# Layer 1's normalised input kept in memory, denominators gathered before the reciprocal, and small steps moved to ScalarE

## The chip, the cores and the metric

The kernel runs on one core of one Trainium2 chip. The metric is the device time of one execution in microseconds, the median of several runs; lower is better. TensorE (PE), VectorE (DVE), ScalarE (ACT), GpSimd (POOL) and the queue of SyncE (SP), which issues nearly all DMA transfers, each work through their own instructions in order.

## What is computed

The input x has 32 images of 1024 channels, 14 x 14 positions each, in float32. `_gn` is a group norm with 32 groups and no weights.

```python
# layer 0
x = x + conv(_gn(x))      # three codebook stages: scores against 16 centroids, softmax,
                          # a product with a table; each followed by a batch norm _bn;
                          # relu between them, and at the end relu(out + identity)
# layer 1
x = x + attn(_gn(x))
# attn(x):
q = elu(wq @ x[:, :512] + bq) + 1;  k = elu(wk @ x[:, 512:] + bk) + 1
qr, kr = rope(q), rope(k)                     # per head: 16 heads of 64
z = 1.0 / (einsum(q, k.mean(-1)) + 1e-06)     # one denominator per head and position
out = einsum(qr, einsum(kr, x) / n) * z
return out + depthwise3x3(x) + lepe_b         # "lepe"
```

The end of layer 0 is `x + relu(bn3(out3) + gn(x))`: layer 1 begins from x, from the normalised x, and from the third stage's output, once the third batch norm's scale and bias are known.

## The kernel before

Layer 0 (the function `layers`) has three stages. Stage 1 normalises each pair of images on ACT (`normalise`, one piece per 128 channels), from 2 images and all 1024 channels at a time; it keeps only the per-image scale `gn_a` and bias `gn_b`, and not the normalised x. Stage 3 works in 14 chunks of 448 positions (`group(k, n)` computes half of the output channels of a chunk) and stores its output in the DRAM tensor `o3d`; at its end a flag says whether the softmaxes overflowed (then an exact version runs in a branch), and `bn_final` computes scale `sc3` and bias `bi3` of the third batch norm.

Layer 1 works on 16 pairs of images (`pair`). The order of its instructions is written by a planner in the kernel's source (`Plan`): each step is given an engine, a rank, a duration, and what it reads and writes; the planner lists the ready step of the lowest rank on every engine, and its result is a fixed order on each engine. The ranks are sums of the constants in `due`, plus `T` times the number of the pair; they set the order alone. Ring buffers (`ring`) limit how far a pair runs ahead of another: three of `x`, four PSUM banks `mm` for products and transposes, four `pa` for attention outputs.

The steps of a pair, for each half h of the channels (1 serves k, 0 serves q):

- `load`: x, and the third stage's output (`o3q`), from DRAM by SP.
- `front`: for each 128 channels ACT computes the normalised x plus `bi3` (`tb` = `gn_b` + `bi3`; two instructions, one per image, L1680) into a PSUM bank; DVE adds the third stage's output times `sc3` (L1689), then `x + max(.., 0)` (L1694), then takes statistics (L1699).
- `group_norm`: DVE sums the statistics, PE averages over a group with the matrix `gavg` (L1734), DVE subtracts and squares, PE averages again, DVE adds epsilon, POOL computes the power of -1/2 and the products (`scale`, `middle`).
- `normalise`: ACT writes the normalised `y` (L1792) and later the scaled x of the residual with the 3x3 filter's centre (L1792).
- `channels`: the q and k products on PE (L1826), relu and exp on ACT (L1835, L1838), the sum on DVE (L1842), totals of k on ACT (L1846).
- `rope`: four POOL steps for each quarter of q and k (L1870 to L1877).
- `v_tokens`, `k_tokens`, `products`: transposes on PE (L1888), copies by ACT, products k by v (L1925).
- `normalisers`: PE computes the denominators (L1976) in 64 rows, of which 16 are needed; ACT adds 1e-6 (L1985); DVE takes the reciprocal of all 128 x 196 (L1993); SP stores it to `zd` (L1988). `normalise_q` spreads the rows over partitions by four transfers into `zb` (L2005), and POOL multiplies q by them (L2012). The last pair does this with PE instead.
- `attend`: the attention product into the four `pa` banks (L2031); `lepe`: eight filter taps per 128 channels on DVE, into the same bank (L2049), and the addition to x (L2063). In four of eight channel blocks (`SIDES`) one tap is done by ACT (L2078) and POOL (L2086) instead (`side_tap`); in the last pair three, and for six blocks the other five by PE (`diagonal_taps`, L2105).
- `store`: the half's result to the output.

The q and k weights (8 x 512 KB in small pieces, L531 to L534) replace the tables of stage 3 in SBUF, so they are loaded at the start of layer 1, in 24 transfers.

Of the kernel before, what the change touches and what calls it, by code (L numbers as in the profile page):

```python
# [17 lines left out]
P = 128  # L18
# [31 lines left out]

class Plan:
# [31 lines left out]
    def write(self):  # L83
# [6 lines left out]
        engines = {p[0] for p in self.pieces}  # L90
# [59 lines left out]
def conv_preact_kernel(ctx: ExitStack, tc: tile.TileContext, a: dict, out: bass.AP):  # L150
# [18 lines left out]
    o3d = dram.tile([P, CT, NTOK], F32, tag="o3d", name="o3d")  # L169

# [250 lines left out]
    bi3 = cp.tile([P, CT], F32, tag="bi3", name="bi3")  # L421

# [118 lines left out]
    def layers(exact, early=None):  # L541
# [281 lines left out]
        with ExitStack() as s:  # L823
# [40 lines left out]

            first = lambda p: 8 * p - 15 if p > 1 else -99
# [16 lines left out]
            for p in range(NP):  # L882
                for c in range(CT):
                    at(8 * p + c - AHEAD - 1 - (p == 0), normalise(p, c))
            at(24, edges)
# [245 lines left out]
        with ExitStack() as s:  # L1131
# [260 lines left out]
            def group(k, n):  # L1392
# [82 lines left out]
                for i in range(2):  # L1475
                    add(os[i][:, 0], high[i], os[i][:, 0])
                both(lambda i, _, w: term(low[i][:, left], table(two, w), inputs(x4), False))
                both(lambda i, _, w: product(low[i], luts[7][:, w], rows[7], stop=True))
# [7 lines left out]
                for i, m in enumerate(ms):  # L1486
                    add(os[i][:, 1], low[i], os[i][:, 1])
                    nc.sync.dma_start(o3d[:, m :: 4, k * NC : (k + 1) * NC], os[i])
                for i, m in enumerate(ms):
                    stats(m + 4, os[i][:, 1], k, not more)  # L1490
                for f in steps[1:3]:
                    f()
                pending.extend(steps[3:])

            for k in range(1, NCH):
# [6 lines left out]
                group(k, 0)  # L1502
                if check:
                    check = check()
                group(k, 1)
                if check:
                    again = check()
            bn_final(once, None, 3, range(CT), sc3, bi3, mv3)
# [20 lines left out]
    with ExitStack() as s:  # L1529
# [14 lines left out]
        tb = once.tile([P, CT, B], F32, tag="tb", name="tb")  # L1544
        nc.vector.tensor_tensor(tb, gn_b, bc(bi3, 2, B), ALU.add)
# [41 lines left out]
        T = 81.22  # L1587
        SIDES = [0, 3, 4, 7]
        ATT = 2.0
# [9 lines left out]
        tiles["o3q"] = []  # L1599
        for n, k in (("zb", 4), ("e", 2)):  # L1600
            ring(n, k, [P, N2])
# [19 lines left out]
        for n, shape in (  # L1621
            ("gst", [P, 8, 6]),
            ("nmc", [P, 8]),
            ("gd", [P, 8, 2]),
# [11 lines left out]
        def load(p, h, rank):  # L1636
# [14 lines left out]
            if p > 0:  # L1651
                do(SP, rank - 12, 0.9, quad, (), [(xt, c) for c in range(4)], lag=5.0)
            os = []
            for k in range(2):
                ot = Slot("qr" if p == 0 and h == 0 else "o3q")
# [7 lines left out]
                else:  # L1663
                    r = rank - 11 + 8 * k if p > 0 else -99
                    do(SP, r, 0.45, third, (), [(ot, 0), (ot, 1)], lag=4.5)
                os.append(ot)
            return xt, os

        def front(p, h, c, xt, ot, rank):

            ch = 4 * h + c
            w = Slot("pa" if p == 0 and c % 2 else "mm")
            xc = lambda: xt()[:, c]
            o = lambda: ot()[:, c % 2]
            wv = lambda: w()[:, :N2]

            def scaled():
                for i in range(2):
# [5 lines left out]
                        bias=tb[:, ch, b : b + 1],  # L1684
# [8 lines left out]
            def added():  # L1693
                nc.vector.scalar_tensor_tensor(xc(), wv(), 0.0, xc(), ALU.max, ALU.add)  # L1694
# [7 lines left out]
            do(ACT, rank, 0.92, scaled, [xk], [w])  # L1702
            do(DVE, rank, 0.54, third, [ok], [w])
            do(DVE, rank, 0.54, added, [w], [xk])
            do(DVE, rank, 0.56, stats, [xk], [("gst", p % 2, h, c)])

        def warm(n, need):
            pw = Slot("mm")

            def piece():  # L1710
                for _ in range(n):
# [3 lines left out]
                        tb.rearrange("p c b -> p (c b)"),  # L1715
# [4 lines left out]
            do(PE, -50, 0.4 * n, piece, need, [pw])  # L1720

        def group_norm(p, h, rank):
# [10 lines left out]
            def average(ps):  # L1733
                return lambda: nc.tensor.matmul(ps()[:, :8], gavg, g("gs"), start=True, stop=True)  # L1734
# [4 lines left out]
            def centred():  # L1739
                for t in (g("gd"), pd()):  # L1740
                    nc.vector.tensor_tensor(t, mean, bc(pm()[:, :8], 2, 2), ALU.subtract)
                nc.vector.tensor_tensor(pd(), g("gd"), pd(), ALU.mult)
                nc.vector.scalar_tensor_tensor(
                    g("gq"), m2, 1.0 / 98.0, pd(), ALU.mult, ALU.add
                )
                halves(g("gq"))
                nc.vector.tensor_scalar(g("nmc"), pm()[:, :8], -1.0, None, ALU.mult)

            def variance():
                nc.vector.tensor_scalar(g("gve"), pv()[:, :8], EPS, None, ALU.add)  # L1750
# [5 lines left out]
            def middle():  # L1756
# [5 lines left out]
                    v(g("xbi")), v(g("xbi")), bc(lb[:, 4 * h : 4 * h + 4], 2, 2), ALU.add  # L1762
# [4 lines left out]
            do(PE, rank, 0.21, average(pm), [key("gs")], [pm], lag=0.3)  # L1767
            do(DVE, rank, 0.65, centred, [pm, *gst], [key("gs"), key("nmc")])
            do(PE, rank, 0.21, average(pv), [key("gs")], [pv], lag=0.3)
            do(DVE, rank, 0.1, variance, [pv], [key("gve")])  # L1770
            if p == 0 and h == 1:

                for n, need in ((12, []), (9, [key("gve")])):
                    warm(n, need)
# [40 lines left out]
        def channels(p, keys, j, r, t, sums, rank):  # L1815
# [42 lines left out]
            do(ACT, rank - 20, 0.49, relu, [pq], [e])  # L1858
            do(ACT, rank - 20, 0.46, exp, [], [e])
            do(DVE, rank - 20, 0.54, greater, [pq, e], [(t, r)])  # L1860
            if keys:
                do(ACT, rank, 1.08, total, [(t, r)], [(sums, r, j)])
# [457 lines left out]
```

## Time and profile before

| | us |
|---|---|
| median of 3 runs (lowest, highest) | 3338.13 (3337.95, 3338.33) |
| profiled execution, whole | 3338.64 |
| its span, first to last instruction | 3336.5 |
| last product of layer 0 on PE ends | 2267.6 |
| first q or k product of layer 1 | 2306.1 |
| last q or k product of layer 1 ends | 3287.6 |

Busy time of the engines over the whole span: PE 3242.5 us (97%), DVE 2841.2 (85%), POOL 2538.4 (76%), ACT 1787.1 (54%). The 40 slices of the profile are 83 us each; the last 13 are layer 1, where DVE and POOL show 9 tenths and ACT 8 or 9.

A group of instructions is shown as: line, engine, operation, output<-inputs, shapes, count | busy time, mean ns of one | idle time of the engine just before them and what ended it. The mean of one counts from start to end; neighbours overlap, so the distance between starts is shorter. A row of the timeline or the chain begins with its start and length in us. A row of windows gives for each engine the busy time and, in brackets, the number of instructions, then the granted PE clock, the share of the DMA engines and GB/s.

### The profile page before, as it was taken

What the parts mean: (1) busy time and instruction counts of PE and PEld (TensorE: products, weight loads), DVE (VectorE), ACT (ScalarE), POOL (GpSimd) and SP (SyncE); (2) the same over time, 40 slices, a digit from 0 to 9 for tenths busy, and PEclk for the clock granted to TensorE, in tenths of its full rate; (3) what the DMA queues carried; (4) which work ended last, traced back from release to release, by engine and by line L of the source; (5) the groups of instructions that cost most, each with busy time, mean ns of one, the idle gap of its engine ahead of it and who ended that gap; (6) DMA issues with size and microseconds to landing.
All of it is one profiled execution on the core that took longest, in us unless ns stands there. A gap on an engine that the chain in (4) does not pass through costs nothing. (4 is left out here: it accounts for less than half of the span.)

```text
span 3336.5 us, 60995 instructions
## 1 busy us (share of the span) xinstructions
PE 3242.5 (97%) x22169; PEld 1974.6 (59%) x22169; DVE 2841.2 (85%) x4191; ACT 1787.1 (54%) x4435; POOL 2538.4 (76%) x1590
## 2 busy tenths in 40 slices
PE   8999999999899999999999999997999999999998
PEld 4555555555354444444478888885666666666665
DVE  8999999997788899888666666754699999999996
ACT  5555555554444444444321111104898898898886
POOL 6999999997788888888532222222989999999998
PEclk9999999999999999999999999998999999999999
DMA  4110110102444444343221111114133333333331
GB/s 122 47 49 28 47 47 28 47 28 77 137 127 119 116 119 125 110 127 107 77 71 50 40 60 48 50 50 116 55 85 95 98 88 93 99 92 89 98 91 40
DMA packets 260493, 266.32 MB, mean 80 GB/s; under 512 B 52077, under 2 KB 258965, under 8 KB 260185
## 3 DMA queue, kind: packets, MB, share of 16 engines
q1 hardware_dynamic: 259488, 262.02, 27.2%
q8 instruction: 178, 2.92, 0.4%
q14 instruction: 131, 1.07, 0.1%
q10 hardware_dynamic: 696, 0.31, 0.0%
HBM read 171.01 MB, written 75.58 MB: 74 GB/s over the span
## 5 line engine op out<-in xcount | busy, mean ns | idle before, releaser
L660 POOL TENSOR_TENSOR t<-t,r 128x1568 f32<-128x1568 f32 (+3 forms) x288 | 961.5, 3339 | 521.2 <-issue 244.5
L780 PE MATMUL po<-t,lut 128*128 128x392 f32 x3840 | 1332.5, 500 | 7.4 <-DMA t<-spare 6.4
L780 PEld LDWEIGHTS po<-t,lut 128*128 128x128 f32 x3840 | 710.7, 190 | 606.6 <-issue 82.5
L1826 PE MATMUL mm<-y,lut 128*128 128x392 f32 x2048 | 706.9, 496 | 4.6 <-DVE k L1842 3.5
L622 DVE STREAM_TRANSPOSE tt<-t 128x1568 f32<-128x1568 f32 (+1 forms) x284 | 517.4, 1822 | 155.0 <-ACT t L610 149.7
L610 ACT ACTIVATE t<-sc,cbias 128x392 f32<-128x392 f32 (+1 forms) x624 | 322.0, 597 | 559.0 <-PE sc L943 187.6
L1826 PEld LDWEIGHTS mm<-y,lut 128*128 128x128 f32 x2048 | 375.6, 188 | 268.3 <-DVE k L1842 10.6
L653 DVE STREAM_TRANSPOSE r<-rc 128x1568 f32<-128x1568 f32 (+1 forms) x284 | 520.8, 1834 | 11.6 <-POOL t L660 1.2
L2049 DVE SCALAR_TENSOR_TENSOR pa<-y,lepe_w,pa 128x406 f32<-128x406 f32 x900 | 527.7, 635 | 2.1 <-PE pa L2031 1.9
L625 POOL TENSOR_TENSOR tt<-tt 128x784 f32<-128x784 f32 x256 | 470.5, 1838 | 31.6 <-DVE tt L622 31.6
L610 ACT ACTIVATE t<-sc,room 128x392 f32<-128x392 f32 x512 | 258.7, 588 | 395.6 <-issue 168.4
L1406 PE MATMUL po<-t,lut 128*128 128x224 f32 (+2 forms) x1352 | 313.3, 414 | 0.0
L641 DVE TENSOR_REDUCE sm<-tt 128x98 f32<-128x784 f32 (+1 forms) x284 | 293.6, 1034 | 1.1 <-POOL tt L625 0.8
L1406 PEld LDWEIGHTS po<-t,lut 128*128 128x128 f32 (+1 forms) x1352 | 233.4, 189 | 62.9 <-issue 60.2
L643 DVE RECIPROCAL rc<-sm 128x98 f32<-128x98 f32 (+1 forms) x284 | 220.1, 775 | 9.8
L664 ACT ACTIVATE sm<-sm 128x98 f32<-128x98 f32 (+1 forms) x284 | 85.3, 300 | 154.8 <-DVE rc L643 154.8
L1680 ACT ACTIVATE mm<-x,tb,gn_a 128x196 f32<-128x196 f32 x248 | 126.9, 516 | 48.8 <-POOL y L1559 28.4
L2012 POOL TENSOR_TENSOR qr<-qr,zb 128x784 f32<-128x784 f32 x64 | 118.3, 1862 | 37.2 <-DMA zb<-zd 37.2
L1838 ACT ACTIVATE e<-e 128x392 f32<-128x392 f32 x256 | 133.5, 521 | 0.7
L1073 PE MATMUL sc<-patch,room 27*32 27x392 f32 x4096 | 122.7, 505 | 8.7 <-DMA patch<-h1d 8.7
L1419 DVE TENSOR_TENSOR o<-po,o 128x224 f32<-128x224 f32 (+1 forms) x156 | 81.6, 543 | 56.7 <-PE po L1406 51.9
L854 ACT ACTIVATE x<-x,gn_b,gn_a 128x196 f32<-128x196 f32 x256 | 127.6, 559 | 0.0
(211 smaller groups left out, 4379.3 us busy)
## 6 DMA issues: line engine op xcount, KB each, us to landing
patch<-h1d SPq DMA_DIRECT2D x383, 108.5 KB
x<-in_x_dram SPq DMA_DIRECT2D x32, 784.0 KB
o3d<-o SPq DMA_DIRECT2D x56, 448.0 KB
x<-in_x_dram SPq DMA_DIRECT2D x64, 392.0 KB
out_dram<-x SPq DMA_DIRECT2D x64, 392.0 KB
o<-o3d SPq DMA_DIRECT2D x62, 392.0 KB
h1d<-pad SPq DMA_DIRECT2D x96, 225.0 KB
patch<-h1d SPq DMA_DIRECT2D x383, 54.2 KB
```

Of the source, the lines that this page charges most:

```text
L610: nc.scalar.activation(t[:, j, : sc.shape[1]], sc, AF.Identity if exact else AF.Exp, bias=bias[:, j : j + 1],)
L622: nc.vector.transpose(tt, tf)
L625: nc.gpsimd.tensor_tensor(tv[:, :, :8], tv[:, :, :8], tv[:, :, 8:], ALU.add)
L641: nc.vector.tensor_reduce(sm, tv, AX.X, ALU.add)
L643: nc.vector.reciprocal(rc, sm)
L653: nc.vector.transpose(r, bc(rc, 2, KC))
L660: nc.gpsimd.tensor_tensor(v[:, c], v[:, c], r[:, c], ALU.mult)
L780: nc.tensor.matmul(po[h], luts[b][:, j, h * P : (h + 1) * P], ts[u % len(ts)][:, j, :N2], start=(b == 0 and j == j0), stop=(b == 7 and j = ...
L1406: nc.tensor.matmul(dst, w, x, start=start, stop=stop)
L1826: nc.tensor.matmul(pv(), w[kt][:, m0 : m0 + P], ywin(p, first + kt), start=(kt == 0), stop=(kt == 3),)
L1838: nc.scalar.activation(e(), e(), AF.Exp, scale=-1.0)
L2049: nc.vector.scalar_tensor_tensor(acc, neighbours(p, c, offset(k)), lw[:, c, k : k + 1], acc, ALU.mult, ALU.add,)
```

## The change

1. Stage 1 of layer 0 also stores the normalised x of pairs 1 to 15 in a DRAM tensor `gnd` (`keep`, 60 transfers of 392 KB by SP). Layer 1 loads it (`kept`, four transfers a pair into a ring `gn` of four) in place of recomputing it with ACT; only pair 0 still does that. `third` adds into the SBUF tile.
2. `bi3` is no longer added to the input of the relu: `x + max(v, -bi3)` is formed, which is the wanted value less `bi3`. Group norm takes account of it by one more matmul per mean (`centring`, L1813 of the new kernel), and `lbi` = `lepe_b` + `bi3` puts it back into the residual.
3. In group norm the square, the negated mean and the added epsilon go from DVE to ACT; one copy of the differences goes.
4. Denominators: ACT's result is stored to `zr`; a transfer gathers the 16 rows that count as 128 x 49 (`zc`); DVE takes the reciprocal of that; it is stored to a smaller `zd`, from which the four spreads are made as before.
5. In pairs before the last, three channel blocks in place of four have a side tap: one tap per pair goes from ACT and POOL back to DVE. The last pair's split is as before.
6. At the end of layer 0 the last chunk's sums are finished in another order with the flag read in between, and scale and bias of the third batch norm are computed in two halves (`last_bn`), nearly all on POOL.
7. All ranks (`due`, `T`) and some durations that the planner assumes are new, several steps have ranks of their own, the k weights come ahead of the `o3d` loads at the start, and the planner goes through the engines in a fixed order. 11 idle matmuls instead of 21 stand at the start (`warm`).

```diff
+            def keep(p, c):
+                def piece():
+                    nc.sync.dma_start(
+                        gnd[:, c - 1 : c + 1, p * N2 : (p + 1) * N2], xts[p][:, c - 1 : c + 1]
+                    )
+                return piece
...
                     at(8 * p + c - AHEAD - 1 - (p == 0), normalise(p, c))
+                    if p > 0 and c % 2:
+                        at(8 * p + c - AHEAD, keep(p, c))
...
+            def last_bn(n):
...
+                nc.vector.tensor_scalar(ve, four(mv3[:, :, 1]), EPS, None, ALU.add)
+                half = mhalf[:, :4].rearrange("p (h m) -> p h m", h=2)
+                nc.gpsimd.tensor_tensor(sc, ve, half, ALU.pow)
+                nc.gpsimd.tensor_tensor(sc, sc, four(g), ALU.mult)
+                nb = four(nbi3)
+                nc.gpsimd.tensor_tensor(ve, four(mv3[:, :, 0]), sc, ALU.mult)
+                nc.gpsimd.tensor_tensor(nb, ve, four(b), ALU.subtract)
+                nc.gpsimd.tensor_tensor(bi, four(b), ve, ALU.subtract)
...
-        tb = once.tile([P, CT, B], F32, tag="tb", name="tb")
-        nc.vector.tensor_tensor(tb, gn_b, bc(bi3, 2, B), ALU.add)
+        nc.vector.scalar_tensor_tensor(centring, gavg, 2.0, ident, ALU.mult, ALU.subtract)
+        nc.gpsimd.tensor_tensor(lbi, lb, bi3, ALU.add)
...
-        SIDES = [0, 3, 4, 7]
+        SIDES = [5, 6, 7]
...
+                def kept(gt=gt, q=q):
+                    nc.sync.dma_start(gt(), gnd[:, 2 * q : 2 * q + 2, p * N2 : (p + 1) * N2])
...
-                nc.vector.scalar_tensor_tensor(xc(), wv(), 0.0, xc(), ALU.max, ALU.add)
+                nc.vector.scalar_tensor_tensor(
+                    xc(), wv(), nbi3[:, ch : ch + 1], xc(), ALU.max, ALU.add
+                )
...
-            do(ACT, rank, 0.92, scaled, [xk], [w])
+            if p == 0:
+                do(ACT, rank, 0.92, scaled, [xk], [wk])
...
             def centred():
-                for t in (g("gd"), pd()):
-                    nc.vector.tensor_tensor(t, mean, bc(pm()[:, :8], 2, 2), ALU.subtract)
-                nc.vector.tensor_tensor(pd(), g("gd"), pd(), ALU.mult)
...
-                nc.vector.tensor_scalar(g("nmc"), pm()[:, :8], -1.0, None, ALU.mult)
+                nc.vector.tensor_tensor(pd(), mean, bc(pm()[:, :8], 2, 2), ALU.subtract)
+            def squared():
+                nc.scalar.activation(pd(), pd(), AF.Square)
+                nc.scalar.activation(g("nmc"), pm()[:, :8], AF.Copy, scale=-1.0)
...
-                nc.vector.tensor_scalar(g("gve"), pv()[:, :8], EPS, None, ALU.add)
+                nc.scalar.activation(g("gve"), pv()[:, :8], AF.Identity, bias=eps)
...
+            do(SP, rank + due["z"], 0.45, keep, ["z"], [("zr", p % 2)], lag=2.3)
+            do(SP, rank + due["z"], 0.45, gather, [("zr", p % 2)], ["zc"], lag=2.3)
+            do(DVE, rank + due["z"], 0.4, recip(zc), [], ["zc"])
+            do(SP, rank + due["z"], 0.45, scatter, ["zc"], [("zd", p % 2)], lag=2.3)
...
-            do(SP, b - 90, 0.95, weights4[b], (), [("w", b)], lag=3.5 + b)
+            do(SP, b - (110 if b < 4 else 90), 1.85, weights4[b], (), [("w", b)], lag=4.5)
```

## The prediction

> **What bounds the kernel now.** I read the busy shares of the 40 slices first, to find the stage that the change touches (layer 1, from 2270 us to the end), then the chain of waits to see its rhythm, then one period of it by engine.
>
> In the chain of waits (start, length, what):
>
> ```profile
> 2579.94 18.71 PE mm L1826 x56
> 2603.07 4.94 DVE pa L2049 x9
> ...
> 2632.67 4.39 DVE pa L2049 x8
> 2637.59 2.20 DVE pa L2049 x4
> 2641.94 18.72 PE mm L1826 x56
> ```
>
> The same pattern returns every 62.0 us, once for each pair of images, and the chain changes between PE (the q and k products, L1826) and DVE (the 3x3 taps, L2049). The busy time of each engine in the next period:
>
> ```profile
> core 0: us, PE busy (x) PEld busy (x) DVE busy (x) ACT busy (x) POOL busy (x), PEclk, DMA share, GB/s
> 2641.94:2703.93 61.99, 60.39 (x616) 39.01 (x617) 60.87 (x134) 55.01 (x138) 57.60 (x55) 1.00 0.34 94
> ```
>
> DVE is idle for 1.1 us of 62.0, PE for 1.6. So two engines bound the period; taking 8 us from ACT alone buys nothing here. The groups of that period which the change touches:
>
> ```profile
> L1680 ACT ACTIVATE mm<-x,tb,gn_a 128x196 f32<-128x196 f32 x16 | 8.2, 516 | 0.3
> L1689 DVE SCALAR_TENSOR_TENSOR mm<-o,sc,mm 128x392 f32<-128x392 f32 x8 | 5.0, 622 | 0.0
> L1694 DVE SCALAR_TENSOR_TENSOR x<-mm,x 128x392 f32<-128x392 f32 x8 | 4.4, 554 | 0.0
> L2086 POOL TENSOR_TENSOR x<-x,side 128x392 f32<-128x392 f32 x4 | 4.1, 1026 | 0.6 <-ACT side L2078 0.6
> L1993 DVE RECIPROCAL z<-z 128x196 f32<-128x196 f32 x1 | 1.4, 1370 | 0.0
> L1734 PE MATMUL mm<-gs,gavg 128*128 128x8 f32 x8 | 1.3, 240 | 0.0
> ```
>
> The start of the stage, in order of time:
>
> ```profile
> 2277.91 1.07 ACT L1680 ACTIVATE mm<-x,tb,gn_a 128x196 f32<-128x196 f32 x2 [28.41 <-POOL y L1559]
> 2289.18 0.17 DVE L1737 TENSOR_REDUCE gs<-gst 128x8 f32<-128x16 f32 x1
> 2294.10 0.20 POOL L1754 TENSOR_TENSOR gb<-nmc,ga 128x8 f32<-128x8 f32 x1
> 2299.11 0.52 ACT L1680 ACTIVATE mm<-x,tb,gn_a 128x196 f32<-128x196 f32 x1 [13.20 <-DMA x<-in_x_dram]
> 2305.05 3.62 ACT L1792 ACTIVATE y<-x,gb,ga 128x196 f32<-128x196 f32 x8
> 2306.13 15.80 PE L1826 MATMUL mm<-y,lut 128*128 128x392 f32 x40
> ```
>
> Scale and bias of the first half are ready at 2294.3, but y, which uses them, starts at 2305.05: ahead of it in ACT's queue stands L1680 for the second pair, which waits 13.2 us for that pair's x. PE's products start at 2306.1.
>
> The path of the denominators:
>
> ```profile
> 2673.11 1.37 DVE L1993 RECIPROCAL z<-z 128x196 f32<-128x196 f32 x1
> 2674.51 0.34 SPq L1988 DMA_DIRECT2D zd<-z  x1
> 2676.35 2.36 SPq L2005 DMA_DIRECT2D zb<-zd  x4
> 2681.76 1.85 POOL L2012 TENSOR_TENSOR qr<-qr,zb 128x784 f32<-128x784 f32 x1 [1.69 <-DMA zb<-zd]
> ```
>
> **The period, part by part.** ACT: the 16 L1680 go (-8.2), one side tap goes (-0.6, as four channels become three), six small steps of group norm come: about 0.25 each, between nothing and the 0.30 of the smallest ACT row (L664, 98 elements), +1.5. 55.0 becomes 47.7; never the bound. POOL loses one L2086: 57.6 - 1.0 = 56.6.
>
> DVE: one tap more, 0.55 (eight L2049 start 4.38 us apart in all). Of group norm, gd, its product, nmc and gve go; their starts in the timeline lie 0.08, 0.22, 0.07 and 0.07 apart, 0.44, twice: -0.9. The reciprocal works on 49 elements a partition instead of 196: the rows with 98 (775 ns) and 196 (1370 ns) give 6.1 ns an element, so 0.48 us: -0.9. L1689 now reads and writes SBUF instead of PSUM: between 622 and the 554 of L1694, which writes SBUF; I take none of the 0.5 us. 60.9 + 0.55 - 0.9 - 0.9 = 59.6 us. In the written order the two halves between attentions now hold equal DVE work (29.8 and 29.7 us by these durations; before 29.8 and 30.9), and taps stand where DVE waited 0.6 us for the group mean.
>
> PE: two more means per pair (`centring` times `bi3`). Four L1734 means take 1.3 us, 0.33 each: +0.65, between +0.3 (weights already loaded beside) and +0.7. 60.4 becomes 61.05. This speaks against the change, and makes PE the bound.
>
> Here a rule differs from the row. The Trainium skill, "Trainium Kernel Development and Optimization", section Best Practices, says that matmul busy time does not tell the distance from the roofline. The trace agrees in part: 56 L1826 take 18.7 us, 2.67 for eight, while eight followed by other work are booked at 2.9, so some of PE's 60.4 is no work. By the row PE ends at 61.05 or more; by the rule PE can shrink, DVE stays the bound, and the period is 59.6 + 1.1 = 60.7. Upper end: PE keeps its 1.6 us of idle, 62.65. I take 61.3, near the row with little idle, since DVE has 1.7 us of slack to deliver in time. 0.7 us in each of 15 periods: **-10.5 us** (rule -20; upper end +10).
>
> The denominators travel further: ACT's z is stored (zr), gathered (zc), inverted, stored (zd), then spread: two hops more on SP's queue. A store with its wait takes 1.84 us here (2674.51 to 2676.35), the spread 5.4 (2676.35 to 2681.76). The gather isn't in the trace: its pieces are 196 B, and "DMA: Bandwidth & Descriptors", section Specifications, says that below 512 B a transfer isn't at line rate. That rule is against the change. By the row it costs 1.9, by the rule perhaps twice that; the weight loads at 2280 us have pieces of 128 to 256 B and moved 264 GB/s, so I take 2.2. From the end of the denominators' product: 1 + 1.9 + 2.2 + 0.7 + 1.9 + 5.4 = 13 us. In the new order POOL's first L2012 stands behind the first two products of the next pair's k (11.1 us of PE work later, then 2 of ACT and DVE) and 4.9 of POOL work: 18 us. So the detour is covered by rope work, and POOL's present wait of 2.7 us goes. Without that cover it would cost 5 us a pair. Behind these waits on SP stand two `gn` loads, the stores and the next x, which have some 20 us. Price taken: 0. The four `gn` loads per pair, 1.6 MB in 61 us, add 26 GB/s to 94: hidden.
>
> **The first layer.** 60 stores of 0.4 MB (`keep`), 24 MB over the first 1000 us, where 59 GB/s flow and PE is busy for 98%. Each stands behind `t<-spare` on SP, one unit after the normalise that it waits for; what is queued behind is needed four units later. 0, at most +3.
>
> The end of layer 0: the last chunk's first half finishes its sum earlier, and `last_bn` takes one POOL chain (1.65 + four of 0.2) instead of POOL and three DVE steps after the statistics; the flag is read before them. From the last product (2267.6) to bi3 it took 6.3 us; I get 4.8. **-1.5**.
>
> **The start.** x of the second pair is no longer in ACT's queue. The first half's four channels now stand alone on DVE: 4 x 1.7 us from 2277.5, gs at 2284.4; 4.6 us more for the group norm (4.9 before, a little DVE work left out, two hops to ACT put in), y at 2289.5, first product at 2290 instead of 2306; the k weights (2.1 MB at 0.27 MB/us from 2278, now all ahead of the o3 loads) are there at 2288. But then DVE is late: in its order the first k result stands behind `gn` of the second pair, and the second behind its x, which on SP now come after 6.6 and 8.2 MB: 2303 and 2309. Four PSUM buffers fill, and the products wait. Following those queues, the first q product starts near 2325; before it was 2331.4 (2328.8 and one group of 2.64). **-5** beyond the 1.5; between +4 (the loads later by 9 us) and -14 (16 us kept).
>
> **The end.**
>
> ```profile
> 3244.39 1.53 POOL L1870 TENSOR_TENSOR kr<-k,cosq 128x784 f32<-128x784 f32 x1 [0.30 <-DVE k L1842]
> 3320.68 1.90 POOL L2012 TENSOR_TENSOR qr<-qr,zb 128x784 f32<-128x784 f32 x1
> 3329.97 1.03 DVE L2063 TENSOR_TENSOR x<-mm,x 128x392 f32<-128x392 f32 x2
> ```
>
> From the last pair's k rope to 3322.6 POOL never rests (78 us); DVE's last ten taps and the store follow. In the new order those taps come earlier, POOL's own work from that point is 77.8 us, with four side taps last; only additions and the 5.5 us of the store follow: 7 saved. But that k rope stands 4.5 us later against the products' end. **-2**, between -7 and +4.
>
> **Sum**, against the profiled execution (span 3336.5, 3338.64 with what lies around it): -1.5 - 5 - 10.5 - 2 = -19. 3338.6 - 19 = 3319.6; the runs' median is 0.5 lower, so **3319 us**.
>
> **Rivals.**
> - *Only the start and end gain* (chance 0.2): PE keeps 0.9 us of idle, the period stays at 62.0. For: PE gets more work, and its order is fixed. Against: DVE, which it waited for, has 1.3 us less. -8.5: 3330 us.
> - *Slower: the denominators' detour decides* (0.18). Each of the three new-style hops on SP costs 6 us instead of 2. The 13 us become 25; 18 are covered and POOL has 4.7 us of slack in 61.3. It decides from 5.2 us a hop on; at 6, 2.3 us a pair, 15 times: 3319 + 35 = 3354. For: 196 B pieces, loads on the same queue. Against: 1.84 us for the store that is there.
> - Forecast 0.62, own range 3304 to 3331.
>
> That the change does nothing is no case: its instructions differ on every engine.
>
> **How the numbers follow.** A change below 0.2% (6.7 us) can't be told from none here. Faster: 0.60 of the forecast, 0.12 of the first rival, 0.01 of the second: 0.73. Same: 0.02 + 0.08 + 0.02 = 0.12. Slower 0.15. The low end is the rule's period with the start fully kept, rounded in: 3300; the upper end takes in the first rival and the mild half of the second: 3343.
>
> **What would show it.** Periods of the PE groups 61.3 apart (62.0: first rival; above: second, with POOL L2116 waiting for `zb`). DVE near 59.6 and ACT near 48 busy in a period. First product near 2290, first q near 2325, with DVE waits on `gn` and x between. Layer 0 ending within 3 us of before. I am wrong if PE waits on DVE in every period although DVE has slack, or if `gn` loads come late in each pair.

## The result and the profile after

The changed kernel takes 3450.03 us (median of 4 runs, 3441.36 to 3451.65) where the kernel before takes 3338.23 us beside it. The ratio is 1.0328, with a 95% interval of 1.031 to 1.0346: slower by 3.3%. The forecast was 3319 us with a range of 3300 to 3343, so it was wrong in sign and the range was missed. The profiled execution took 3451.19 us, its span is 3449.0 us.

The rhythm of layer 1 is still one pattern per pair of images, but the distance between two patterns is now 71.1 us on the mean (twelve periods from 2435.29 to 3288.20 us) instead of 62.0. The busy times of the engines in two such lengths, 71.91 and 71.85 us, of the changed kernel (window and length, then PE, PE's weight loads, DVE, ACT, POOL with instruction counts, PE clock, DMA share, GB/s):

```profile
core 0: us, PE busy (x) PEld busy (x) DVE busy (x) ACT busy (x) POOL busy (x), PEclk, DMA share, GB/s
2740.99:2812.90 71.91, 63.26 (x621) 40.49 (x620) 70.89 (x127) 48.89 (x126) 60.69 (x54) 0.98 0.35 104
2812.90:2884.75 71.85, 63.23 (x621) 40.43 (x620) 70.83 (x127) 48.90 (x126) 60.63 (x54) 0.98 0.35 104
```

ACT fell from 55.0 to 48.9 us, as forecast (47.7). DVE has 7 instructions fewer than before (127 against 134) and is busy for 10.0 us more: 70.9 of 71.9 us. PE, which was idle for 1.6 us of a period before, now is for 8.6. DVE alone bounds the period now. The chain of waits of the changed kernel agrees: where PE and DVE took turns before, DVE's instructions follow each other (start, length, what).

```profile
2732.55 1.42 DVE gn L1763
2734.50 1.95 DVE gn L1763 x2
2736.45 1.71 issue
2738.16 1.31 DVE gn L1763
2739.47 1.10 DVE pa L2153 x2
2741.10 5.09 DVE pa L2153 x10
2746.50 1.18 DVE pa L2153 x2
2749.30 1.87 DVE x L1768 x2
```

The groups of the first of the two periods above, by line (count, busy us, mean ns of one, idle before):

```profile
L2153 DVE SCALAR_TENSOR_TENSOR pa<-y,lepe_w,pa 128x406 f32<-128x406 f32 x61 | 34.7, 634 | 0.0
L1763 DVE SCALAR_TENSOR_TENSOR gn<-o,sc,gn 128x392 f32<-128x392 f32 x8 | 12.1, 1554 | 0.0
L2116 POOL TENSOR_TENSOR qr<-qr,zb 128x784 f32<-128x784 f32 x4 | 8.0, 2016 | 0.0
L1768 DVE SCALAR_TENSOR_TENSOR x<-gn,nbi,x 128x392 f32<-128x392 f32 x8 | 7.9, 1038 | 0.0
...
L2092 DVE RECIPROCAL zc<-zc 128x49 f32<-128x49 f32 x1 | 0.5, 451 | 0.0
```

Here the time is. L1763 is the old L1689 (sum of the third stage's output and the normalised input) and L1768 the old L1694 (maximum, plus x). They took 5.0 + 4.4 = 9.4 us per pair; now they take 12.1 + 7.9 = 20.0 us, 10.6 us more, with the same number of elements. The taps L2153, the same operation over slightly more elements, still take 634 ns. What differs is where the inputs lie: the taps have one input in SBUF (y) and one in PSUM (pa), and so had the two old steps (`mm` was in PSUM). Now both inputs of both steps lie in SBUF. POOL became slower as well: L2116 takes 2016 ns where L2012 took 1854 in the period that the prediction shows, and POOL is busy for 60.7 us instead of 57.6.

Over the whole changed kernel L1763 is the main new loss, and PE's wait for DVE its consequence (the page's groups):

```profile
L1917 PE MATMUL mm<-y,lut 128*128 128x392 f32 x2048 | 738.0, 511 | 39.8 <-DVE q L1933 38.3
...
L1763 DVE SCALAR_TENSOR_TENSOR gn<-o,sc,gn 128x392 f32<-128x392 f32 x120 | 160.5, 1376 | 8.4 <-DMA gn<-gnd 5.9
```

The path of the denominators in the changed kernel, in order of time:

```profile
2711.00 0.34 SPq L2079 DMA_DIRECT2D zr<-z  x1
2712.90 0.54 SPq L2083 DMA_DIRECT2D zc<-zr  x1
2716.98 0.45 DVE L2092 RECIPROCAL zc<-zc 128x49 f32<-128x49 f32 x1
2717.46 0.33 SPq L2087 DMA_DIRECT2D zd<-zc  x1
2721.41 2.34 SPq L2109 DMA_DIRECT2D zb<-zd  x4
2728.94 1.86 POOL L2116 TENSOR_TENSOR qr<-qr,zb 128x784 f32<-128x784 f32 x1
```

The five hops take longer than forecast (10.4 us from the first store to the spread), but POOL starts its first multiplication without a wait for `zb`: no idle time is shown in its row, none in the group L2116 above, and in the whole trace no L2116 waits for `zb`.

The start and the end of layer 1 in the changed kernel:

```profile
2288.61 2.76 ACT L1883 ACTIVATE y<-x,gb,ga 128x196 f32<-128x196 f32 x6 [2.03 <-POOL gb L1843]
...
2294.31 4.34 PE L1917 MATMUL mm<-y,lut 128*128 128x392 f32 x8
...
2297.21 1.16 DVE L1763 SCALAR_TENSOR_TENSOR gn<-o,sc,gn 128x392 f32<-128x392 f32 x2 [3.40 <-DMA gn<-gnd]
...
2336.74 0.62 DVE L1933 SCALAR_TENSOR_TENSOR q<-mm,qbu,e 128x392 f32<-128x392 f32 x1
...
3437.20 4.20 POOL L2190 TENSOR_TENSOR x<-x,side 128x392 f32<-128x392 f32 x4
```

y starts at 2288.6 and the first product at 2294.3, 11.8 us earlier than before, but the first q result is there at 2336.7, and in the trace of before it is there at 2336.3: the whole gain is gone by then. One more thing is in the third of these rows. At 2297 us, when POOL does nothing (from 2296.1 to 2299.8 us), two L1763 with both inputs in SBUF take 1.16 us together, as before. So two SBUF inputs alone are not slow; something has to run beside them.

**The theories.** Theory A: a DVE instruction with two SBUF inputs and a POOL instruction that reads SBUF hold each other up. The Trainium skill, "SBUF — State Buffer", section Who interferes with whom, says that a VectorE instruction with two SBUF inputs contends with a GpSimd instruction that reads SBUF, because its second input comes through a read port that the two engines share; and that one with at most one SBUF input (outside VectorE's two-port modes), or a `tensor_reduce`, doesn't. POOL is busy for 60 of 72 us with `tensor_tensor` instructions, all of which read SBUF. Rival B: the new ranks put the work in an order that is bad for DVE. Rival C: the loads of `gn` come late or disturb. Rival D: the longer way of the denominators through memory (the detour) costs the time.

### The profile page after: what moved, and what is told of

The parts are those of the page before. It is cut to its first block, busy times and chain, and to the rows that moved or that the text cites. A ratio compares the mean times of both kernels' runs of the same rounds, so it can differ in the third digit from the quotient of the medians.

```text
span 3449.0 us, 60974 instructions
## 1 busy us (share of the span) xinstructions
PE 3284.5 (95%) x22213; PEld 2001.1 (58%) x22213; DVE 2958.3 (86%) x4077; ACT 1696.1 (49%) x4276; POOL 2580.2 (75%) x1585
## 5 line engine op out<-in xcount | busy, mean ns | idle before, releaser
L1917 PE MATMUL mm<-y,lut 128*128 128x392 f32 x2048 | 738.0, 511 | 39.8 <-DVE q L1933 38.3
L1917 PEld LDWEIGHTS mm<-y,lut 128*128 128x128 f32 x2048 | 384.3, 194 | 317.8 <-DVE q L1933 48.0
L2153 DVE SCALAR_TENSOR_TENSOR pa<-y,lepe_w,pa 128x406 f32<-128x406 f32 x915 | 520.5, 633 | 13.9 <-PE pa L2135 13.9
L1961 POOL TENSOR_TENSOR kr<-k,cosq 128x784 f32<-128x784 f32 x64 | 109.2, 1706 | 105.2 <-DVE gs L1825 60.2
L1937 ACT ACTIVATE unread<-k 128x196 f32<-128x196 f32 x256 | 93.6, 366 | 164.0 <-DVE k L1933 159.7
L1763 DVE SCALAR_TENSOR_TENSOR gn<-o,sc,gn 128x392 f32<-128x392 f32 x120 | 160.5, 1376 | 8.4 <-DMA gn<-gnd 5.9
```

The source lines that it names most:

```text
L1763: nc.vector.scalar_tensor_tensor(wv(), o(), sc3[:, ch : ch + 1], wv(), ALU.mult, ALU.add)
L1917: nc.tensor.matmul(pv(), w[kt][:, m0 : m0 + P], ywin(p, first + kt), start=(kt == 0), stop=(kt == 3),)
L2153: nc.vector.scalar_tensor_tensor(acc, neighbours(p, c, offset(k)), lw[:, c, k : k + 1], acc, ALU.mult, ALU.add,)
```

## Experiments

### The operands alone, outside the kernel

Twelve L77 on DVE in each stage, with nothing beside them, or with POOL products or memsets.

```python
def dve(o, i, j, n):
    for _ in range(n):
        nc.vector.scalar_tensor_tensor(o, i, col, j, ALU.mult, ALU.add)   # L77
def pool(m, n):
    for _ in range(n):
        nc.gpsimd.tensor_tensor(g2[:, :m], g0[:, :m], g1[:, :m], ALU.mult)  # L81
```

> No part of the reference is computed: x is copied to the output while twelve VectorE scalar_tensor_tensor instructions of 128x392 run in each stage, against nothing, against GpSimd tensor_tensor products of 128x392 (about 1.0 us) or 128x784 (about 1.9 us) with two SBUF inputs, or against GpSimd memsets. Theory A (VectorE with two SBUF inputs and GpSimd reading SBUF exclude each other): alone about 0.6 us whatever the operands; with both inputs in SBUF beside 128x392 products about 1.6 us from start to start (0.6 + 1.0), beside 128x784 products about 2.5 us, and the products are stretched likewise; with one input in PSUM 0.55 to 0.65 us in every stage; sum written to PSUM but both inputs in SBUF as slow as both in SBUF. Rival C (loads): no DMA runs here, so 0.6 us in every stage.

The rows for L77 and L81 of the microbenchmark (duration ns as min/median/max, start of the first and the last): both inputs in SBUF, first beside products of 128x392, then beside products of 128x784.

```profile
L77 DVE SCALAR_TENSOR_TENSOR sc<-sa,col,sb x12: 625/1260/1264, 15.1 to 28.1; 128x392 f32<-128x392 f32 x12
...
L81 POOL TENSOR_TENSOR g<-g,g x12: 1008/1216/1383, 15.9 to 30.3; 128x392 f32<-128x392 f32 x12
...
L77 DVE SCALAR_TENSOR_TENSOR sc<-sa,col,sb x12: 625/2084/2087, 32.1 to 52.5; 128x392 f32<-128x392 f32 x12
...
L81 POOL TENSOR_TENSOR g<-g,g x10: 2037/2042/2207, 32.9 to 52.1; 128x784 f32<-128x784 f32 x10
```

And over all stages with one input in PSUM, which were run alone and beside both sizes of products:

```profile
L77 DVE SCALAR_TENSOR_TENSOR pa<-sa,col,pa x36: 621/631/631, 55.5 to 86.0; 128x392 f32<-128x392 f32 x36
L77 DVE SCALAR_TENSOR_TENSOR sc<-pa,col,sc x36: 615/626/627, 91.3 to 121.3; 128x392 f32<-128x392 f32 x36
L77 DVE SCALAR_TENSOR_TENSOR pb<-sa,col,sb x12: 632/1256/1259, 126.7 to 139.7; 128x392 f32<-128x392 f32 x12
```

Alone, or beside memsets, the instruction with two SBUF inputs takes 627 ns. Beside products of 128x392 (1010 ns alone) it takes 1260 ns, beside products of 128x784 (1835 ns alone) 2084 ns. In both cases that is the POOL instruction's own time plus 250 ns, and one DVE instruction comes through per POOL instruction: the ten stretched ones of the first stage start 1.30 us apart ((28.13 - 16.47) / 9), and so do the products beside them. With one input in PSUM nothing is stretched, whatever POOL does. Where the result goes (last row: to PSUM) does not matter. In the changed kernel L1763 on `gn` lies between 607 and 2216 ns, about the two ends found here. The copy of x to the output was on its way for the first 82 us, which the expectation had overlooked; the stage of the last row, from 126.7 us on, has none and is stretched as much, and the stage alone at 6.3 us had it beside it and took 627 ns. So rival C is not needed for the stretch. The expectation had one size wrong: the two do not simply follow each other (627 + 1010 would be 1637 ns from start to start, where 1.30 us is measured), and POOL's products became only 206 ns longer each (1216 instead of 1010). The minimum of 625 ns in the first rows is that of the two instructions that ran before the first product had started.

### The operands alone, inside the kernel before

```diff
-            w = Slot("pa" if p == 0 and c % 2 else "mm")
+            w = Slot("gn" if p > 0 else "pa" if c % 2 else "mm")
...
-        for n, k in (("zb", 4), ("e", 2)):
+        for n, k in (("zb", 4), ("e", 2), ("gn", 4)):
```

> The kernel before, with one edit: from the second pair on ScalarE's L1680 writes a x + b to an SBUF buffer instead of a PSUM buffer, and the sum and the maximum work on it there. No loads, no other change. Theory A: L1689 rises from 0.62 to 1.3 to 1.5 us, L1694 from 0.55 to 0.9 to 1.0, the period from 62.0 to 71 to 73 us, the time to 3338 + 15 x 9.7 = about 3480 (3460 to 3500). Rivals B and C: 3338, within 10 us.

It took 3483.48 us, against 3351.81 for the kernel before beside it: 1.039. (In all these experiments the kernel before takes 3350 to 3352 us, 0.4% more than beside the first result, so ratios are what is to be compared.) Its groups between 2640 and 3280 us, and two periods:

```profile
L1689 DVE SCALAR_TENSOR_TENSOR gn<-o,sc,gn 128x392 f32<-128x392 f32 x71 | 76.8, 1081 | 0.4 <-ACT gn L1680 0.2
L1694 DVE SCALAR_TENSOR_TENSOR x<-gn,x 128x392 f32<-128x392 f32 x71 | 76.2, 1073 | 0.1
```

```profile
2569.73:2642.64 72.91, 62.04 (x615) 39.93 (x613) 70.18 (x134) 55.97 (x141) 64.91 (x61) 0.98 0.28 80
2642.64:2719.66 77.02, 68.22 (x630) 43.66 (x629) 75.18 (x142) 60.85 (x149) 62.82 (x56) 0.93 0.26 76
```

One edit, which moves a buffer from PSUM to SBUF and adds no load and no store, makes the kernel before slower than the changed kernel. Theory A said 3480. The periods are 72.1 us on the mean (thirteen from 2432.18 to 3369.36 us), 10.1 longer than before; the two rows account for 7.8 of them (8 x (1.081 + 1.073 - 0.622 - 0.554)), and DVE's busy time grew by as much (894.04 / 13 = 68.8 us against 60.9). The split between the two steps came out more even than expected (1.08 and 1.07 us instead of 1.4 and 0.95), with about the same sum. Rivals B and C both said 3338. C falls, since no load was added. B does not fall by this run alone: the edit also frees PSUM banks, the planner therefore wrote another order (of DVE's 2037 instructions after 2300 us only 997 are in the same place as before), and the 2.3 us per period that the rows leave open may be that. The next experiment has no such gap.

### One SBUF input in the changed kernel's own order

```diff
             def third():
+                if p > 0:
+                    nc.vector.tensor_reduce(wv()[:, :1], o(), AX.X, ALU.add)
+                    return
...
             def added():
+                if p > 0:
+                    nc.vector.tensor_reduce(xc()[:, :1], wv(), AX.X, ALU.add)
+                    return
```

> The changed kernel with its order of instructions on every engine kept, all loads kept too; only the two steps on gn (sum, and maximum plus x), for the second pair on, are replaced by VectorE tensor_reduce instructions over the same 128x392 operand, which have one SBUF input: the sum over o goes into one column of gn, the sum over gn into one column of x. So the third convolution, the residual addition and the maximum are left out for those pairs. Theory A (two SBUF inputs): the two take about 0.5 us each and are not stretched; VectorE 70.9 - 19.1 + 8.5 = about 60.3 us busy in a period of 61 to 62.5 us instead of 71.9; time 3450 - 15 x 10.4 = about 3294 (3285 to 3315), which also says what the rest of the change brings. Rival B (the new order): the period stays above 66 us, time above 3370. Rival C (gn loads late or in the way): likewise, with VectorE waiting for gn or x in each pair.

It took 3320.38 us (3318.58 to 3325.59); the ratio to the kernel before on the same chip is 0.9909, interval 0.9893 to 0.9926. Its groups between 2640 and 3280 us, and two of its periods:

```profile
L1764 DVE TENSOR_REDUCE gn<-o 128x1 f32<-128x392 f32 x72 | 36.5, 547 | 0.0
L1772 DVE TENSOR_REDUCE x<-gn 128x1 f32<-128x392 f32 x76 | 37.2, 545 | 0.0
```

```profile
2977.50:3037.39 59.89, 59.61 (x617) 39.47 (x609) 59.04 (x127) 48.80 (x127) 56.51 (x54) 1.00 0.42 125
3037.39:3097.53 60.14, 59.25 (x614) 39.39 (x603) 59.09 (x127) 48.64 (x126) 56.54 (x53) 1.00 0.43 124
```

The order of every engine, the loads and the detour are those of the changed kernel, and the loss is not there: from 3.3% slower to 0.9% faster, 4.2% or about 140 us. Up to 16 us of that is no stretch: the two steps take 612 ns each where nothing stretches them (the mean of 617 and 608 in the recompute experiment below), the reduces 546, 1.1 us per pair less. So the stretch is worth 3.7 to 4.2%. This decides against B, C and D as the cause; of D the trace says more: in periods close to the forecast's 61.3 us, POOL never waits for `zb`. The periods are not all as short as these two: from 2424.18 to 3224.82 us thirteen of them take 800.6 us, 61.6 us each. In a long one (64.2 us) PE stands still once for 4.1 us before the denominators' product, with no releaser in the trace; what that is stays open.

### Half of the dose

```diff
             def added():
+                if p > 0:
+                    nc.vector.tensor_reduce(xc()[:, :1], wv(), AX.X, ALU.add)
+                    return
```

> The changed kernel, order and loads kept; only the second step on gn (maximum, plus x) of the pairs from the second on is replaced by a tensor_reduce over gn into one column of x, one SBUF input. The residual addition and the maximum are left out for those pairs. Theory A: eight of the sixteen stretched instructions of a pair are left; L1763 stays at 1.3 to 1.6 us, the replaced one takes 0.55, VectorE 70.9 - 7.2 + 4.4 = about 68 us in a period of about 69; time 3395 to 3420 where the changed kernel takes 3450. If only the first of two neighbours had to wait for GpSimd, L1763 alone would carry it all and the time would stay within 15 us of the changed kernel's.

A single execution: 3385.06 us (the kernel before: 3350.37). L1763 stays at 1517 ns (76 of them between 2640 and 3280 us), the replaced step takes 542, and two periods are

```profile
2759.34:2825.72 66.38, 61.74 (x544) 39.42 (x532) 66.31 (x128) 47.16 (x124) 58.60 (x53) 0.97 0.37 113
2825.72:2893.19 67.47, 62.91 (x746) 41.17 (x748) 66.96 (x129) 50.85 (x130) 60.62 (x55) 1.00 0.36 111
```

With eight of the sixteen stretched instructions DVE is busy for 66.6 us, between the 59.1 of the experiment above and the 70.9 of the changed kernel. The time lies 10 us below the expected range: the step taken out was worth 3.6 us per pair in its own rows (7.9 - 8 x 0.542), but 4.2 us of DVE's busy time. Of the other 0.6 us, L1763 gave 0.3 (8 x (1.554 - 1.517)); the rest was not followed. The other theory of this run, that the first step alone carries the loss, falls.

### The sum in PSUM, with two SBUF inputs left

```diff
-                wk = (gt, c % 2)
-                wv = lambda: gt()[:, c % 2]
+                w = Slot("mm")
+                wk = w
+                wv = lambda: w()[:, :N2]
...
-                    wv(), o(), sc3[:, ch : ch + 1], wv(), ALU.mult, ALU.add
+                    wv(), o(), sc3[:, ch : ch + 1], wv() if p == 0 else gt()[:, c % 2], ALU.mult, ALU.add
```

> The changed kernel, but the sum o*sc+gn is written to a PSUM buffer, so that the first step still has two SBUF inputs and the second (maximum, plus x) has one. Theory A: the first stays near 1.4 us, the second falls from 0.96 to about 0.55, the period from 71.9 to about 68.5 to 69.5, the time to about 3400 to 3415. Rival B (order) and rival C (loads late or in the way): nothing changes, 3440 to 3455.

It took 4528.08 us, which no theory had said, so the total tells nothing about A. The two lines of this kernel (duration ns as min/median/max) still do:

```profile
L1764 DVE SCALAR_TENSOR_TENSOR mm<-o,sc,gn x120: 616/635/2030, 2298.9 to 4332.2; 128x392 f32<-128x392 f32 x120
...
L1769 DVE SCALAR_TENSOR_TENSOR x<-mm,nbi,x x124: 601/615/627, 2279.3 to 4368.8; 128x392 f32<-128x392 f32 x124
```

With one input in PSUM the second step is never stretched (627 ns at most); the first, with two in SBUF, goes up to 2030, with a median of 635, but now POOL is busy for only 274 of the 640 us from 2640 to 3280. The kernel is slow for a different reason. The sum now asks for one of the four `mm` banks, which the products and transposes need too, while the changed kernel's ranks were made without that need, and the engines wait for each other: L1764 waited 105.7 us for ACT's `kv` copies, which empty such a bank, between 2640 and 3280 us. This reading fits the waits; no run separates it.

### Every pair recomputed by ScalarE

```diff
-            if p == 0:
-                w = Slot("pa" if c % 2 else "mm")
-                wk = w
-                wv = lambda: w()[:, :N2]
-            else:
-                wk = (gt, c % 2)
-                wv = lambda: gt()[:, c % 2]
+            w = Slot("pa" if p == 0 and c % 2 else "mm")
+            wk = w
+            wv = lambda: w()[:, :N2]
...
-            if p == 0:
-                do(ACT, rank, 0.92, scaled, [xk], [wk])
+            do(ACT, rank + (due["third"] if p > 0 else 0), 0.92, scaled, [xk], [wk])
```

> The changed kernel, but every pair takes the path of the first one: ScalarE computes the normalised input into PSUM (16 L1680-like instructions a pair back), the sum and the maximum have one PSUM input each, and neither the stores of layer 0 nor the loads of gn are there. Theory A (operands in SBUF): the two steps back at 0.62 and 0.55 us, VectorE near 60 us busy in a period of 61 to 62 us, time 3338 - 36 + 15 x (-0.7) = about 3292, at most 3320. Rival B (the new order of the queues): the period stays above 70 us and the time above 3430. Rival D (the denominators' detour): the period stays some us above 62, with GpSimd waiting for zb; above 3340.

It took 3429.41 us; ratio 1.0228, interval 1.0211 to 1.0245. The two steps are back at 617 and 608 ns, as A said, and yet it is nearly as slow as the changed kernel. Three periods in sequence:

```profile
2701.33:2764.57 63.24, 57.56 (x574) 37.02 (x563) 49.58 (x106) 51.42 (x135) 56.35 (x54) 1.00 0.30 87
2764.57:2836.63 72.06, 65.12 (x755) 42.10 (x753) 67.59 (x143) 55.25 (x140) 57.97 (x55) 1.00 0.30 85
2836.63:2910.09 73.46, 64.21 (x550) 41.01 (x554) 63.29 (x133) 61.24 (x154) 56.05 (x53) 0.91 0.28 82
```

No engine is full over the three together: DVE is busy for 180 of 209 us, PE for 187. A's time for this run (3292) was wrong, because it took for granted that the changed kernel's order also suits the old buffers. What is left is rival B, for this kernel: the order does not suit the buffers. The next experiment puts that to the test.

### The same instructions in an order fitted to them

```diff
-        T = 139.7
-        SIDES = [5, 6, 7]
+        T = 157.0
+        SIDES = [3, 5, 7]
...
-            third=-61.6,
-            stats=-43.2,
+            third=-153.67,
+            stats=95.72,
...
+            recompute=-46.25,
```

(Nearly all other ranks change too.)

> The same instructions as in the first recompute experiment (every pair's normalised input computed by ScalarE into PSUM, all other parts of the change kept, no stores and loads of gn), but with ranks fitted to that: the order in which the planner lists the steps is new, and the channel blocks 3, 5 and 7 have the side tap. Theory A with order as the second cause: neither step on PSUM is stretched (0.62 and 0.61 us), and the periods of 62 to 75 us of the first recompute experiment shrink to 61 to 62.5; ratio to the kernel before 0.995 to 1.000. If the first recompute experiment was slow for another reason than its order (PE has too much to do, ScalarE too late whatever the order), the periods stay above 65 us and the ratio above 1.015.

3344.90 us against 3350.37 us of the kernel before on that chip: ratio 0.9982, interval 0.9972 to 0.9991 (11 and 15 runs). So with the instructions of the last experiment and another order (and the side taps in other blocks), 2.5% (82 us) are gone, and the order was what made that kernel slow. It is faster than the kernel before by 0.2%, at the edge of what can be told: the single profiled executions, 3340.0 us here and 3339.6 us for the kernel before, show nothing. Its periods are about 63 us long, with DVE busy for 60.2. POOL waits in them for `zb`, 19.7 us in 560 us, which is no more than in the kernel before (22.8), so the detour of the denominators doesn't explain them; what holds them at 63 us was not followed.

The profile of the kernel before, taken beside this one:

> The kernel before without any edit, for a trace from the same chip as these runs: periods of 62.0 us, L1689 at 0.62 us and L1694 at 0.55 us, 3338 to 3356 us.

3339.6 us, periods of 62.0 us with DVE busy for 60.9 in them: the trace the prediction was made from repeats on this chip. This execution is shorter than all 15 that were timed beside it (3347.02 to 3357.15 us), and none of those was traced; so differences of 0.3% between two traces say nothing.

### Parts of the change put into the kernel before

The denominators' detour alone (`zr`, `zc`, smaller `zd`, as in the change):

> The kernel before with one part of the change: the denominators go through memory before the reciprocal (store, gather to 49 elements a partition, reciprocal, store, spread). Price by the prediction's step: VectorE loses 0.9 us a pair; the hops are covered or not by what stands ahead of the first multiplication on GpSimd in this order; 3328 to 3342 on the scale where the kernel before takes 3338 (ratio 0.997 to 1.001). Rival D (the detour decides): GpSimd waits 5 us or more for zb in each pair, period 65 to 67 us, ratio 1.015 or more. Rival B: the planner, which sees other lags, gives another order, and that alone makes some us a pair.

3355.37 us against 3351.39: ratio 1.0013, interval 1.0004 to 1.0021. That is a loss of at most 0.2%, and no gain; the periods take turns at 61.1 and 65.5 us. DVE has less to do, as forecast, and POOL waits 22.1 us for `zb` in 560 us, as much as in the kernel before (22.8). The forecast of 5 us or more per pair by rival D is excluded for this order too.

With the small steps of group norm on ACT as well (square, negated mean, epsilon):

> The same as the last, and the small steps of group norm on ScalarE too (square, negated mean, variance plus eps); no gn path, no centring product, all else as in the kernel before. By the prediction's step: VectorE 60.9 - 0.9 - 0.9 = 59.1 us busy, PE 60.4, ScalarE 56.5; period 61.0 to 61.8 instead of 62.0; ratio 0.995 to 0.999. Rival B (order): the planner's order differs on every engine from that of the kernel before, and the period is longer than 63 us although no engine has more work; ratio 1.005 or more.

3379.05 us: ratio 1.0089, interval 1.0072 to 1.0106. DVE is busy for less than before, PE has no more products, and the periods are near 65 us:

```profile
2817.82:2882.82 65.00, 61.71 (x613) 39.98 (x612) 60.58 (x129) 56.89 (x145) 57.49 (x55) 0.97 0.32 90
2882.82:2947.62 64.80, 62.23 (x622) 41.32 (x621) 58.38 (x123) 55.08 (x141) 57.12 (x55) 0.97 0.31 90
```

That is what rival B said of this run. Which of the new waits of PE makes the 3 us was not separated, so "the order" is here the best reading, not a shown one. In these two runs taking work from DVE, with the ranks as they were, brought nothing.

## Why the prediction was wrong, point by point

**The step that failed** is in the period, in DVE's part: "L1689 now reads and writes SBUF instead of PSUM: between 622 and the 554 of L1694, which writes SBUF; I take none of the 0.5 us." The move was costed as a matter of where the result goes. What counts is where the inputs come from, and what POOL does meanwhile. L1689 and L1694 together were taken at 9.4 us per pair and measure 20.0. Put into the forecast's own sum, DVE is 59.6 + 10.6 = 70.2 us, and 70.9 is what the trace shows; with it DVE, not PE, bounds the period. The upper bound of the step was missing: the row of L1694, taken as the nearest, has one PSUM input and could not show the resource. The trace of before held the signs: a POOL busy for 57.6 of 62.0 us with instructions that read SBUF, and, outside the stage that the prediction read, two lines of layer 0 with two large SBUF inputs on DVE (duration ns as min/median/max, start of the first and the last):

```profile
L1267 DVE TENSOR_TENSOR x<-t,x x13: 841/842/1603, 1684.3 to 2223.1; 128x672 f32<-128x672 f32 x13
L1269 DVE TENSOR_TENSOR x<-t,x x13: 857/858/1805, 1685.9 to 2224.0; 128x672 f32<-128x672 f32 x13
```

Twelve of the thirteen times nothing runs on POOL and they take 0.84 and 0.86 us. The first time, at 1684 and 1686 us, they meet POOL instructions that read SBUF (L1246 to L1248) and take 1.60 and 1.80 us. So the cost could be read from the kernel before, by asking for its longest durations instead of its means. The section cited above speaks against the change too, and the prediction looked at neither. With them, 16 instructions that each wait for half to the whole of a POOL instruction (57.6 us / 55 = 1.05 us on the mean) would have given an estimate of 8 to 17 us more per pair.

**The rest of DVE's sum was right.** With one SBUF input in each (the experiment that replaces both steps) DVE is busy for 59.1 us. The forecast was 59.6, less 16 x (0.588 - 0.546) = 0.7 us for the shorter instructions: 58.9. The reciprocal (0.45 us, forecast 0.48) is part of that. One term is missing from the sum: the second step, with a column in place of the constant 0, takes 608 ns even with a PSUM input (the recompute experiment; 554 before), 0.4 us per pair. The fitted recompute experiment, which keeps that step, has DVE busy for 60.2 us, and 59.6 + 0.4 is 60.0. ACT's 47.7 became 48.9. POOL's 56.6 is 56.5 without the stretch, and 60.7 with it.

**PE, row against rule.** The row said 61.05 us of PE work and a period of 61.3, the rule that busy time is no distance to the limit said 60.7. Without the stretch PE's busy time fell to 59.4 us in the periods of 60 us although it has more products, so the rule was nearer in those; the mean of 61.6, with the long ones in it, is near the row. Neither matters in the changed kernel.

**The start** was half wrong. The first product came 11.8 us earlier (16 forecast). DVE's waits for `gn` (3.40 and 2.49 us), for x (2.82) and for `o` (2.53) stand where they were put. But their sum was underrated. The first q product, forecast near 2325, starts at 2330.0 (2331.4 before), and the first q result comes at 2336.7 us instead of 2336.3, so nothing of the 5 us is left there. The stretch is only a part of that: in the experiment with one SBUF input the product starts at 2329.4 and the result comes at 2333.5, 2.8 us earlier than before, which is about what the end of layer 0 gave.

**The end of layer 0** gave 2.6 us (bi3 at 2271.3 instead of 2273.9; 1.5 forecast; 0.6 of it because the last product ends earlier, at 2267.0 instead of 2267.6), and the stores of `keep` cost nothing that can be seen. **The last pair** can't be judged in the changed kernel, where DVE is late everywhere. In the experiment with one SBUF input POOL's last side tap ends at 3310.6 of 3318.3 us: 7.7 us before the end, where before it was 13.9. That is the form that the step described.

**The denominators' detour** was priced at 0 and costs 0 in this order, for the reason given: it is covered. The changed kernel's long periods alone would not show that, but POOL waits for `zb` nowhere in the experiment with one SBUF input either. The slower rival, six microseconds a hop, did not come: the store took 1.9 us, the gather with the wait about 4, the second store 3.95. That the kernel is slower is not to its credit, since it named another mechanism. What the detour costs where it isn't covered no run shows by itself.

**A gain that was there, and a loss that ate it.** By the experiment with one SBUF input, the order, loads and small steps of the change are worth 0.4 to 0.9%; the two steps' second SBUF input costs 3.7 to 4.2%. The forecast without the step that failed was 19 us, 0.6%. That its size agrees is in part luck, since the start, which was to give 5 of the 19, gave none.

## What to carry to other kernels

Before a VectorE operand is moved from PSUM to SBUF, count the SBUF inputs of the instruction and look at what GpSimd does beside it: here a second SBUF input cost 0.63 us each time beside GpSimd instructions of 1.01 us, and 1.46 us beside those of 1.84. An instruction with one PSUM input was never stretched, and an extra ScalarE pass that puts the input there, as in the kernel before, was the cheaper way. And an order fitted to one set of buffers is no base for trying another: a part taken alone can look worthless or harmful because the order no longer fits.

## What the runs showed of the hardware

- A VectorE instruction with two SBUF inputs doesn't simply take turns with GpSimd: it takes about 250 ns more than the GpSimd instruction it meets takes alone (1260 ns for 1010, 2084 for 1835), while GpSimd loses only about 0.2 us each time. An exclusive lock for the whole of each instruction, as the section cited above has it, would put 0.63 + 1.01 = 1.64 us between two starts; measured are 1.30. The measurement is milder than the page. Whether the lock is held for less than the recorded length of an instruction was not separated.
- A `tensor_reduce` over 128x392 in SBUF took 561 ns at most (545 on the mean) beside a GpSimd that was busy for 56 of 60 us: not stretched at all.
- PE's granted clock tended to be lower where PE waited more, without a fixed relation. In the kernel before it is 1.00 in each period, with PE busy for 97%; it is 0.98 in the two periods of the changed kernel shown above (PE busy for 88%), 0.91 in the last of the three periods of the first recompute experiment (87%), but 1.00 in the two before that (91% and 90%). Over the whole of the run with 4528 us it is 0.859, and one product took 572 ns there on the mean, where the kernel before has 496. So a stage that starves PE can pay for it a second time; what decides it was not tested.
